# Loads of a batched residual matmul: two lines of a sample in one 8 KB piece, for four lines in one of 16 KB

## The chip, the cores and the metric

The kernel runs on one core of one Trainium2 chip. The metric is device time in microseconds of one execution of the whole program, the median of several; lower is better. The profile is of one such execution, recorded by the hardware profiler.

## The reference

There are 128 samples, each a matrix of 128 channels by 1024 points, and 8 weight matrices of 128 by 128, all in float32. Each sample has a subject number from 0 to 7. The sample is multiplied by its subject's weights, and the product is added to the sample.

```python
def reference(x, itok_B_0_7, L0_cond_weights):
    # x: (128, 128, 1024), itok_B_0_7: (128,) int32 in 0..7, L0_cond_weights: (8, 128, 128)
    w = L0_cond_weights[itok_B_0_7]
    return x + jnp.einsum('bct,bcd->bdt', x, w)
```

A sample is 512 KB, so the input and the output are 64 MiB each: every byte of them is read once and written once.

## The kernel before

**Tiles and slots.** The work is cut into 64 tiles of two samples (`G = 2`), 1 MB each. A tile lives in one of 23 slots of SBUF (`xs`, `SLOTS = 23`): the load fills the slot, the sum overwrites it in place, and the store reads it. A slot is therefore taken from the issue of its load to the landing of its store. Channels lie on the 128 partitions, so that a partition holds 4 KB of each sample.

**Loads.** SP issues them, two to a tile (L138, one for each sample), through the helper `transfer`, whose instruction carries the line L57. The sample in memory is 128 lines of 4 KB, one after the other. The load names them as 32 pieces of four lines (`ROWS = 4`, L142), so that one piece of 16 KB is contiguous in memory and is spread over four partitions. In the first 23 tiles the load of tile i waits until tile i-3 has landed (`LEAD = 3`, L136); later it waits until the store of the tile that had the slot before has landed (L134). A DMA that has landed adds 16 to its slot's semaphore, one from each of the 16 DMA engines.

**Arithmetic.** When both loads of a tile have landed, TensorE does eight matmuls of 128x128 by 128x512 into one of two PSUM buffers (L171). GpSimd copies each sample's weight matrix out of the eight on the chip ahead of time, by the subject number (L165). VectorE adds PSUM and the slot in one instruction for the tile (L181).

**Stores.** ACT waits for the sum and issues one store of 1 MB for the tile (L183, again with the line L57 of the helper). A store is 128 pieces of 8 KB on the side of SBUF: one partition's two samples lie side by side there. ACT does nothing else, so that a store waits only for its sum and for stores ahead of it on ACT's queue.

**Order.** There is no planner: each engine runs its own instructions in the order of the program, and semaphores tie them. Loads are on one hardware queue (SP's) and stores on another (ACT's); both feed the same 16 DMA engines. At the end SP waits for the last 23 stores (L192).

Of the kernel before, what the change touches and what calls it, by code (L numbers as in the profile page):

```python
# [1 line left out]

# [4 lines left out]

F32 = mybir.dt.float32
I32 = mybir.dt.int32
ALU = mybir.AluOpType


G = 2

N = 512  # L30

SLOTS = 23

W_SLOTS = 4
P_SLOTS = 2

R = 8
DMA = 16

TURN = DMA * (G + 1)  # L40

LEAD = 3

IDLE = 3

ROWS = 4
QUEUES = {mybir.EngineType.SP: "qSPDynamicHW", mybir.EngineType.Activation: "qActDynamicHW"}


def transfer(nc, engine, out, in_):  # L50

    later, nc._always_lower_symbolic_ap = nc._always_lower_symbolic_ap, False
    ins, outs = engine.lower_ap_dma(in_), engine.lower_ap_dma(out)
    nc._always_lower_symbolic_ap = later
    return engine.add_instruction(  # L57
        mybir.InstDMACopy(
            name=nc.get_next_instruction_name(),
            engine=engine.engine,  # L60
            ins=ins,
            outs=outs,
            mode="Copy",
            cce_op=ALU.bypass,
            queue=QUEUES[engine.engine],
        )
    )


@with_exitstack  # L70
def kernel(
    ctx: ExitStack,
    tc: tile.TileContext,
    x: bass.AP,
    subjects: bass.AP,
    weights: bass.AP,
    out: bass.AP,
):
    nc = tc.nc
    B, C, T = x.shape  # L80
    S, _, D = weights.shape
    NT = B // G

    def sbuf(name, *shape, dtype=F32):
        return ctx.enter_context(nc.sbuf_tensor(name, list(shape), dtype)).ap()

    given, near, wrap, index = (
        sbuf(name, 1, B, dtype=I32) for name in ("given", "near", "wrap", "index")
    )
    w_all = sbuf("w_all", C, S, D)  # L90
    ws = [sbuf(f"w{i}", C, 1, D) for i in range(W_SLOTS)]
    zeros = sbuf("zeros", C, N)
    xs = [sbuf(f"x{i}", C, G, T) for i in range(SLOTS)]
    ps = [
        ctx.enter_context(nc.psum_tensor(f"ps{i}", [D, G, T], F32)).ap() for i in range(P_SLOTS)
    ]

    s_given = tc.alloc_semaphore("s_given")
    s_wall = tc.alloc_semaphore("s_wall")
    s_index = tc.alloc_semaphore("s_index")  # L100
    s_zeros = tc.alloc_semaphore("s_zeros")
    s_copied = tc.alloc_semaphore("s_copied")
    s_product = tc.alloc_semaphore("s_product")
    s_added = tc.alloc_semaphore("s_added")
    s_slot = [tc.alloc_semaphore(f"s_slot{i}") for i in range(SLOTS)]

    with tc.tile_critical():  # L107

        nc.scalar.dma_start(given, subjects.rearrange("(o b) -> o b", o=1)).then_inc(s_given, DMA)

        nc.vector.memset(zeros, 0.0).then_inc(s_zeros, 1)  # L111
        nc.tensor.wait_ge(s_zeros, 1)
        for _ in range(IDLE):
            nc.tensor.matmul(  # L114
                ps[P_SLOTS - 1][:, G - 1, :N], zeros[:, :D], zeros, start=True, stop=True
            )

        nc.vector.wait_ge(s_given, DMA)  # L120
        nc.vector.tensor_scalar(near, given, -S, S - 1, ALU.max, ALU.min).then_inc(s_index, 1)  # L121
        nc.vector.wait_ge(s_index, 1)
        nc.vector.tensor_scalar(wrap, near, 0, S, ALU.is_lt, ALU.mult).then_inc(s_index, 1)  # L123
        nc.vector.wait_ge(s_index, 2)
        nc.vector.tensor_tensor(index, near, wrap, ALU.add).then_inc(s_index, 1)  # L125
        nc.gpsimd.wait_ge(s_index, 3)

        nc.sync.dma_start(w_all, weights.rearrange("s c d -> c s d")).then_inc(s_wall, DMA)  # L130
        for i in range(NT):
            k, turn = i % SLOTS, i // SLOTS
            if turn:
                nc.sync.wait_ge(s_slot[k], TURN * turn)  # L134
            elif i >= LEAD:
                nc.sync.wait_ge(s_slot[k - LEAD], DMA * G)  # L136
            for g in range(G):
                transfer(  # L138
                    nc,
                    nc.sync,  # L140
                    xs[k][:, g, :],
                    x[i * G + g].rearrange("(a r) t -> a (r t)", r=ROWS),  # L142
                ).then_inc(s_slot[k], DMA)

        nc.gpsimd.wait_ge(s_wall, DMA)
        for i in range(NT):
            k, turn = i % SLOTS, i // SLOTS
            p = ps[i % P_SLOTS]
            nc.tensor.wait_ge(s_slot[k], TURN * turn + DMA * G)
            if i >= P_SLOTS:  # L150
                nc.tensor.wait_ge(s_added, i - P_SLOTS + 1)
            for g in range(G):
                b = i * G + g
                if b % R == 0:
                    _, subject = nc.values_load_multi_w_load_instructions(
                        index[0:1, b : b + R],
                        engines=[mybir.EngineType.Pool],
                        min_val=0,
                        max_val=S - 1,
                        skip_runtime_bounds_check_because="the index is clamped on the chip above",  # L160
                    )
                w = ws[b % W_SLOTS]
                if b >= W_SLOTS:
                    nc.gpsimd.wait_ge(s_product, b - W_SLOTS + 1)
                nc.gpsimd.tensor_copy(w, w_all[:, bass.ds(subject[b % R], 1), :]).then_inc(  # L165
                    s_copied, 1
                )

                nc.tensor.wait_ge(s_copied, b + 1)
                for t in range(0, T, N):  # L170
                    mm = nc.tensor.matmul(  # L171
                        p[:, g, t : t + N],
                        w[:, 0, :],
                        xs[k][:, g, t : t + N],
                        start=True,
                        stop=True,
                    )
                mm.then_inc(s_product, 1)

            nc.vector.wait_ge(s_product, (i + 1) * G)  # L180
            nc.vector.tensor_tensor(xs[k], p, xs[k], ALU.add).then_inc(s_added, 1)  # L181
            nc.scalar.wait_ge(s_added, i + 1)
            transfer(  # L183
                nc,
                nc.scalar,
                out[i * G : (i + 1) * G].rearrange("g d t -> d g t"),
                xs[k].rearrange("d (o g) t -> d o (g t)", o=1),
            ).then_inc(s_slot[k], DMA)


        for i in range(NT - SLOTS, NT):
            nc.sync.wait_ge(s_slot[i % SLOTS], TURN * (i // SLOTS + 1))  # L192


# [1 line left out]
_INS = ["x", "itok_B_0_7", "L0_cond_weights"]  # L196
_OUTS = [((128, 128, 1024), "float32")]


# [20 lines left out]
```

## Time and profile before

| what | value |
|---|---|
| median of 3 runs | 327.43 us (327.18 to 327.75) |
| the profiled execution | 327.53 us |
| its span in the profile | 325.5 us |
| moved by DMA in the span | 134.85 MB, mean 414 GB/s |
| TensorE matmuls busy | 241.3 us, 74% of the span |
| VectorE busy | 147.9 us, 45% |
| GpSimd busy | 37.6 us, 12% |
| loads of x | 128 of 512 KB |
| stores | 64 of 1 MB |

The span reaches from the first instruction of the program to the last one in the profile; the execution's own time is 2.0 us longer, which lies outside. The page's slices cut the span into 40 equal parts of 8.1 us; a digit is the busy share of an engine in tenths. The trace also has a record for each DMA packet, with its queue, its size, its start and the time that it took: q1 is SP's queue and q10 ACT's. A packet of 4 bytes is the update of a semaphore. In the chain of waits, a line gives start, duration and what the time was spent on.

### The profile page before, as it was taken

How to read it: one execution, taken by the hardware profiler on the slowest of the kernel's cores; microseconds unless marked ns; L12 is line 12 of the kernel's file. 1: busy time of each engine (PE TensorE's matmuls, PEld its weight loads, DVE VectorE, ACT ScalarE, POOL GpSimd, SP SyncE). 2: the span in 40 equal slices, each digit the busy share in tenths (PEclk: the TensorE clock that was granted, in tenths of full speed). 3: DMA queues.
4: the chain of work that ended last, by engine and by line, in shares of the span. 5: the costliest groups of instructions: out<-in, count | busy, mean ns of one | idle time of the engine just before them, and what ended most of it. 6: DMA issues, size and time to landing. Idle time of an engine off the chain costs nothing.

```text
span 325.5 us, 1703 instructions
## 1 busy us (share of the span) xinstructions
PE 241.3 (74%) x518; PEld 95.2 (29%) x518; DVE 147.9 (45%) x68; POOL 37.6 (12%) x132
## 2 busy tenths in 40 slices
PE   6999998987989999989889889887777878000000
PEld 2444433332333333333333333332232332000000
DVE  1475765554555555555555555555354336100000
POOL 1111111111111111111111111111101110000000
PEclk9999999999999999999999999999999979755555
DMA  7999999999999999999999999999999999999994
GB/s 258 411 419 431 419 435 415 420 428 419 427 431 421 431 419 429 416 424 428 423 427 423 420 428 422 428 421 431 421 433 435 417 419 422 429 424 429 424 429 191
DMA packets 16410, 134.85 MB, mean 414 GB/s; under 512 B 3089, under 2 KB 4114, under 8 KB 4114
## 3 DMA queue, kind: packets, MB, share of 16 engines
q1 hardware_dynamic: 7184, 67.64, 49.6%
q10 hardware_dynamic: 9218, 67.11, 49.2%
q8 instruction: 4, 0.07, 0.1%
q14 instruction: 4, 0.03, 0.0%
HBM read 67.63 MB, written 67.11 MB: 414 GB/s over the span
## 4 chain that ended last, share of the span: by engine, by line
DMA 44%; SPq 23%; another core or an unknown queue 15%; PE 2%; issue 1%; DVE 1%
DMA x<-in_x_dram 29%; SPq L57 23%; DMA out_dram<-x 14%; PE ps L171 2%; DVE x L181 1%; SPq L130 0%; SPq L216 0%; SPq L107 0%
## 5 line engine op out<-in xcount | busy, mean ns | idle before, releaser
L171 PE MATMUL ps<-x,w 128*128 128x512 f32 x512 | 235.9, 607 | 32.5 <-DMA x<-in_x_dram 32.5
L181 DVE TENSOR_TENSOR x<-ps,x 128x2048 f32<-128x2048 f32 x64 | 146.7, 2292 | 128.0 <-PE ps L171 128.0
L171 PEld LDWEIGHTS ps<-x,w 128*128 128x128 f32 x512 | 93.4, 191 | 175.6 <-issue 97.3
L165 POOL COPY w<-w_all 128x128 f32 x128 | 37.4, 294 | 230.6 <-PE ps L171 224.6
L114 PE MATMUL ps<-zeros 128*128 128x512 f32 x6 | 5.4, 1076 | 1.7 <-DVE zeros L111 1.7
L114 PEld LDWEIGHTS ps<-zeros 128*128 128x128 f32 x6 | 1.8, 326 | 3.8 <-issue 2.1
L111 DVE MEMSET zeros<- 128x512 f32 x1 | 0.5, 485 | 1.1 <-SPq L107 1.1
L121 DVE TENSOR_SCALAR near<-given 1x128 int32<-1x128 int32 x1 | 0.2, 216 | 0.7 <-DMA given<-in_itok_B_dram 0.7
L125 DVE CUSTOM_DVE_ANT_0 index<-near,wrap 1x256 uint16<-1x256 uint16 x1 | 0.3, 280 | 0.0
L123 DVE TENSOR_SCALAR wrap<-near 1x128 int32<-1x128 int32 x1 | 0.2, 216 | 0.0
L207 POOL MEMSET const-float32-0.0<- 128x1 f32 x1 | 0.1, 98 | 0.2 <-issue 0.2
L207 POOL MEMSET const-bfloat16-1.0<- 128x1 bf16 x1 | 0.1, 101 | 0.0
L207 POOL MEMSET const-uint8-127<- 128x1 uint8 x1 | 0.1, 101 | 0.0
L207 POOL MEMSET const-float32-1.0<- 128x1 f32 x1 | 0.1, 98 | 0.0
## 6 DMA issues: line engine op xcount, KB each, us to landing
x<-in_x_dram SPq DMA_DIRECT2D x128, 512.0 KB, 11.8
out_dram<-x ACTq DMA_DIRECT2D x64, 1024.0 KB, 41.6
w_all<-in_L_cond_weights_dram SPq DMA_DIRECT2D x1, 512.0 KB, 4.4
given<-in_itok_B_dram ACTq DMA_DIRECT2D x1, 0.5 KB
```

The lines of the kernel that those rows point to most:

```text
L57: return engine.add_instruction(mybir.InstDMACopy(name=nc.get_next_instruction_name(), engine=engine.engine, ins=ins, outs=outs, mode="Cop ...
L111: nc.vector.memset(zeros, 0.0).then_inc(s_zeros, 1)
L114: nc.tensor.matmul(ps[P_SLOTS - 1][:, G - 1, :N], zeros[:, :D], zeros, start=True, stop=True)
L121: nc.vector.tensor_scalar(near, given, -S, S - 1, ALU.max, ALU.min).then_inc(s_index, 1)
L123: nc.vector.tensor_scalar(wrap, near, 0, S, ALU.is_lt, ALU.mult).then_inc(s_index, 1)
L125: nc.vector.tensor_tensor(index, near, wrap, ALU.add).then_inc(s_index, 1)
L165: nc.gpsimd.tensor_copy(w, w_all[:, bass.ds(subject[b % R], 1), :]).then_inc(s_copied, 1)
L171: mm = nc.tensor.matmul(p[:, g, t : t + N], w[:, 0, :], xs[k][:, g, t : t + N], start=True, stop=True,)
L181: nc.vector.tensor_tensor(xs[k], p, xs[k], ALU.add).then_inc(s_added, 1)
L207: nc = _bacc.Bacc("TRN2", target_bir_lowering=False, num_devices=1)
```

## The change

The constant `ROWS` goes from 4 to 2. A load then names a sample as 64 pieces of two lines, 8 KB each, and each piece is spread over two partitions. Issuing engine, queue, order, waits, slots and the number of loads stay as they are, and so do the stores and all arithmetic.

```diff
--- before
+++ after
@@ -43,7 +43,7 @@
 
 IDLE = 3
 
-ROWS = 4
+ROWS = 2
 QUEUES = {mybir.EngineType.SP: "qSPDynamicHW", mybir.EngineType.Activation: "qActDynamicHW"}
```

The only use of it is in the load's access pattern (L142), which is not edited:

```python
                    x[i * G + g].rearrange("(a r) t -> a (r t)", r=ROWS),
```

## The prediction

> **What bounds the kernel now.** I read the page's slices first, then the DMA queues over chosen stretches, then the end of the chain of waits. The slices:
>
> ```profile
> PE   6999998987989999989889889887777878000000
> DMA  7999999999999999999999999999999999999994
> GB/s 258 411 419 431 419 435 415 420 428 419 427 431 421 431 419 429 416 424 428 423 427 423 420 428 422 428 421 431 421 433 435 417 419 422 429 424 429 424 429 191
> ```
>
> DMA is full in every slice except the first and the last. TensorE's last six slices are empty: all multiplying is over at 275 us, and 50 us of stores follow. So no engine's arithmetic sets the end; it is set by how long 16 DMA engines take for 134.85 MB, and by whether they are ever left without work. The trace's packet records add up: the first data packet starts at 2.07 us, the packets of the two hardware queues took 321.6 us per DMA engine, the last one ends at 323.64, and the span closes at 325.5. 2.07 + 321.6 + 1.9 = 325.5: no idle time between.
>
> Next, who gets the DMA engines. q1 holds the loads (SP), q10 the stores (ACT). The queues over 30 to 210 us, and over 230 to 270 us:
>
> ```profile
> q1 hardware_dynamic: 4191, 45.82, 60.3%
> q10 hardware_dynamic: 4196, 30.48, 40.5%
> ...
> q10 hardware_dynamic: 1171, 8.54, 50.8%
> q1 hardware_dynamic: 771, 8.44, 50.0%
> ```
>
> The columns are packets, MB, share of the engines. In the first stretch the packets are equal (4191 and 4196) and the bytes are not (1.50 to 1). Per DMA engine a load of 512 KB is two packets of 16 KB and one of 4 bytes for the semaphore: 3 packets for 32 KB. A store of 1 MB is eight packets of 8 KB and one of 4 bytes: 9 packets for 64 KB. One packet each in turn gives 32/3 against 64/9, which is 1.50. So **turns go by packet, the semaphore's included**. In the second stretch the loads no longer have their turn every time: they have run 23 tiles ahead, SP waits for slots (L57 behind stores), and bytes are equal. That lead is the 50 us of stores at the end, and it hides the last tile's arithmetic, which the chain shows:
>
> ```profile
> 263.62 8.05 DMA x<-in_x_dram
> 271.67 0.04 issue
> 271.72 3.71 PE ps L171 x8
> ...
> 275.46 2.29 DVE x L181
> ```
>
> The last load lands at 271.67, its sum is done at 277.75, and its store waits in ACT's queue until 301.35.
>
> [...]
>
> **The change part by part.**
> (1) *Pieces.* Each load is 64 packets of 8 KB for 32 of 16 KB: 4096 more packets over the run, 256 per DMA engine. Bytes, partitions reached and semaphore packets stay. An 8 KB read isn't in the trace; the nearest row is the 8 KB store packet. Means over the run: 311.6 ns for it, 619.1 ns for a 16 KB load packet. 2 x 311.6 - 619.1 = 4 ns, times 256 = 1.0 us, all on the path, since DMA is full. Bounds: 0 if the cost goes by bytes (a 16 KB packet then stands for two of 309.5); 2 x 312.5 - 616.8 = 8.2 ns, 2.1 us, by the means of 30 to 210 us. [...] I take 1.0.
> (2) *Start.* Up to 18 us there are only loads, at 643 ns per 16 KB packet, 27 above that of 30 to 210 us. If that excess belongs to every packet, 22 more packets per engine cost 0.6 us; if to bytes, nothing; if it goes with shorter pieces, -0.6. I take 0 and keep both ends.
> (3) *Issue.* SP issues the same 128 loads (597 ns each, 77 of 325 us). The weight load of 1024 pieces took 0.44 us to issue, so more pieces cost SP nothing visible. ACT, VectorE, GpSimd and TensorE have the same instructions in the same order; no wait is added in the program.
> (4) *Turns.* This is the main term. A load becomes 5 packets for 32 KB per engine, 10 turns per tile, against 9 for the tile's store. With both queues full, stores now move 10/9 of the bytes of loads, not 2/3. Stores can't pass the loads that they depend on, so they catch up. At 18.3 us, when the first store packet runs, 5 tiles have landed; landing to store takes about 8 us (below), 1.6 tiles at 5 us a tile, so some 3.4 tiles of stores are behind. They gain one tile in nine: gone after about 31 of 64 tiles. From then on each store leaves as its tile is ready, loads have the rest, DMA stays full (two to three tiles of loads are always asked for by LEAD), and a tile takes each DMA engine 8 load and 8 store packets, 16 x 311.6 ns = 4.99 us. TensorE needs 3.43 us a tile and VectorE 2.29: neither binds.
> (5) *End.* The loads now finish late, and **the last tile's work is no longer covered**. From the last load packet to its store's first packet: 0.77 to land (270.90 to 271.67), 0.05 to start, 3.74 matmuls (271.72 to 275.46), 2.29 add, 0.03, and 1.1 from issue to first packet (weights: 0.97 to 2.07). Sum 7.98 us. Meanwhile DMA has the store before it, 2.49 us (8 x 311.6), and the rest of the one before that, which started two tiles (9.98 us) earlier, so 2.0 us before the loads ended, and had half the turns: 2.49 - 1.0 = 1.49. Idle: 7.98 - 2.49 - 1.49 = 4.0 us. Low end 3.2: if that store's first packet stood behind 1.5 us of load packets already taken up. High end 7.4: if TensorE's clock is at half for the last tile, as it was after a gap of 2.14 us at 262.56 (matmuls 0.85 us apart for 0.43: 8 x 0.42 = 3.4 more).
> Sum: 1.0 + 0 + 4.0 = +5.0 us: profiled span 330.5, profiled execution 327.53 + 5.0 = 332.5, and 0.1 less for a median of 327.43: **332.4 us**. Its own range is 330.0 (3.2 with pieces at no cost, 0.6 off at the start) to 335.
>
> **Rivals.**
> *Half clock at the end*, 0.13: as above, +3.4: 335.8. TensorE will pause about 1.5 us in every tile, as it did from 230 to 270, where the clock dipped once in eight tiles.
> *The backlog stays*, 0.11: the share is not by turns of single packets once pieces are equal (semaphore packets not counted gives 4 to 4 for equal bytes, no catching up), so stores stay 3 tiles behind and cover the last tile. Only (1) is left: 327.4 to 329.5, likeliest 328.4. Against it: 1.50 needs the semaphores to count; without them it would be 2.
> *Faster*, 0.06: [...] At 304 ns, 512 load pieces per engine save 512 x 5.5 = 2.8 us; it decides only with the backlog kept, since the 4.0 of the end outweighs it, and below some 308 ns (309.5 less 0.65 us over 512 packets): 324.6. For it: only the slower packets of the reads-only start. Against it: half-size store packets show no gain.
> *The piece stays whole or the queue cuts both alike* (no change): the page counts 4096 packets of 16 KB for the loads by difference, so the cut follows the access pattern; 0.02, in "same".
>
> **How the numbers follow.** Main case 0.68, half clock 0.13, backlog kept 0.11, faster 0.06, no change 0.02. Within 0.2% is 0.65 us, about what a measurement of this kernel can tell from no change. Slower: 0.68 + 0.13 + 0.08 of the backlog case = 0.89; same: 0.03 + 0.02 = 0.05; faster 0.06. The range for 8 in 10 goes from 329.3, below the main case and a little into the kept backlog, to 335.9, to the half clock.
>
> **What would show it.** Right: about 8190 load data packets of 8 KB at 310 to 316 ns; equal packets on q1 and q10 early with bytes near 0.9 to 1, then equal bytes; TensorE busy in slices nearly to the end at seven tenths; the last load landing near 319 us instead of 272; SP no longer waiting for stores; two gaps of DMA, about 1.5 and 2.5 us, in the last 12 us. Wrong: a last load before 300 us, or a last stretch of stores back to back; load packets off 308 to 316 ns would put (1) wrong; stores more than one tile behind in the second half would put (4) wrong.

## The result, and the profile after

The changed kernel takes 331.12 us (median of 4, 330.99 to 331.25) against 327.36 us for the kernel before: 3.76 us more, a ratio of 1.011 with a 95% interval of 1.0098 to 1.0122. The forecast was 332.4 us, slower. The profiled execution took 331.2 us with a span of 329.2, so 3.7 us more than the span before; what lies around the span is 2.0 us as before.

The slices of the page, after the change:

```profile
PE   6999667686776868777678677677677687686680
DMA  7999999999999999999999999999999999999964
GB/s 252 412 403 429 426 425 426 424 427 425 420 427 428 422 426 427 426 424 420 427 426 422 428 427 422 424 425 423 426 426 425 425 424 427 426 423 425 424 255 184
```

Up to the 38th slice DMA is as full as before and moves the same 425 GB/s. The loss is in the last two slices: 255 and 184 GB/s, where the kernel before had 429 and 191. TensorE has no empty slice until the last; it multiplies at six to eight tenths nearly to the end.

The queues of the changed kernel, as packets, MB and share of the engines, from 20 to 60 us and from 230 to 270 us:

```profile
q10 hardware_dynamic: 1223, 8.97, 53.2%
q1 hardware_dynamic: 1227, 8.07, 48.1%
...
q1 hardware_dynamic: 1303, 8.54, 51.0%
q10 hardware_dynamic: 1164, 8.49, 50.5%
```

At first the packets are equal again (1223 and 1227), and now the loads have fewer bytes: 8.07 to 8.97 MB, 0.90 to 1, the nine tenths that five packets for 32 KB against nine for 64 KB give. Later the bytes are equal and stores have fewer packets: they have caught up with the loads, and their queue is empty part of the time. A store now lands 9.6 us after its issue (median), where it was 41.6 before.

The end of the chain of waits (start, duration, what), and two short stretches from the table of windows (the stretch, its length, busy time of TensorE, weight loads, VectorE and GpSimd, clock, DMA share, GB/s):

```profile
277.56 39.79 DMA x<-in_x_dram
317.35 0.04 issue
317.39 3.71 PE ps L171 x8
321.11 0.02 issue
321.13 2.29 DVE x L181
```

```profile
317.00:319.60 2.60, 2.21 (x5) 1.06 (x6) 1.45 (x1) 0.00 (x0) 1.00 0.12 47
322.50:324.60 2.10, 0.00 (x0) 0.00 (x0) 0.92 (x1) 0.00 (x0) 1.00 0.00 0
```

The last load lands at 317.35 instead of 271.67. The durations of the matmuls and the sum behind it have not changed, but nothing covers them: while they run, DMA is nearly idle twice, at 47 GB/s and at 0. In the first of the two stretches data still move in one packet at a time from 317.46 on, until 319.32: a single engine is late, and the others have nothing to do. The store of the last tile is issued at 323.45 and its first packet starts at 324.66.

### The profile page after: what moved, and what is told of

It reads as the page before. It is cut to its first block, busy times and chain, and to the rows that moved or that the text cites. A ratio compares the mean times of both kernels' runs of the same rounds, so it can differ in the third digit from the quotient of the medians.

```text
span 329.2 us, 1703 instructions
## 1 busy us (share of the span) xinstructions
PE 240.7 (73%) x518; PEld 94.3 (29%) x518; DVE 147.9 (45%) x68; POOL 37.9 (12%) x132
## 4 chain that ended last, share of the span: by engine, by line
SPq 55%; DMA 39%; issue 1%; PE 1%; DVE 1%
SPq L57 55%; DMA x<-in_x_dram 39%; PE ps L171 1%; DVE x L181 1%; SPq L130 0%; SPq L216 0%; SPq L107 0%
## 6 DMA issues: line engine op xcount, KB each, us to landing
x<-in_x_dram SPq DMA_DIRECT2D x128, 512.0 KB, 35.1
```

## The experiments

Two theories stood against each other. **The lost lead**: with equal turns by packet, smaller load pieces let the stores catch up, so that no stores are left to cover the last tile's matmuls, sum and store. **The cost of pieces**: 4096 more packets make DMA itself slower, 3.7 us in all. Times are medians; ratios are against the kernel before, run on the same chip (327.47 to 327.64 us on the four chips of the experiments).

**1. Win the lead back without touching the loads.** Against the changed kernel, the store names SBUF without joining its two samples, so its pieces are 4 KB:

```diff
-                xs[k].rearrange("d (o g) t -> d o (g t)", o=1),
+                xs[k],
```

> Loads in 8 KB pieces as after the change, stores in 4 KB pieces. By turns of single packets, loads move 32 KB in 5 turns and stores 64 KB in 17, so bytes of loads to stores go 1.70 to 1 and loads run ahead again. Theory of the lost lead (the last tile's work is uncovered because stores catch up): a tail of stores comes back, the last load lands before 275 us, time 327.4 plus 0 to 2 us for the smaller store pieces. Rival, cost of pieces (each 4096 more packets cost 3.7 us of DMA time): at least 331.1, and up to 338 with 8192 more store packets.

Measured: 328.64 us, ratio 1.0029 (1.0019 to 1.0039), 2.5 us faster than the changed kernel although it has 8192 packets more. From 30 to 60 us the queues of this kernel were:

```profile
q1 hardware_dynamic: 1224, 8.04, 63.8%
q10 hardware_dynamic: 1219, 4.67, 37.9%
```

Equal packets, and bytes of 1.72 to 1 where turns give 1.70. The last load landed at 271.76 and a stretch of stores came back. That stretch ran at 421 GB/s from 280 to 320 us (426 in the kernel before), 1.2% less, so pieces of 4 KB have a small cost of their own. That fits the 1.1 us by which the run lies above the kernel before.

**2. Cover the end without touching any packet.** Against the changed kernel, stores are held back for a while near the end (`HOLD = 4`):

```diff
-            nc.scalar.wait_ge(s_added, i + 1)
+            held = max(i + 1, min(i + 1 + HOLD, 60)) if i >= 44 else i + 1
+            nc.scalar.wait_ge(s_added, held)
```

> Loads in 8 KB pieces; from tile 44 on a store is issued only when four more tiles are summed, and from the sum of tile 59 on all are released. This makes a backlog of stores just before the end and alters no packet. Lost lead: the backlog covers the last tile's work, 327.4 to 328.6 us (about 0.5 for a longer stretch of loads alone). Cost of pieces: 331 or more.

Measured: 328.18 us, ratio 1.0021 (1.0014 to 1.0028): 2.9 of the 3.8 us are back, with the same 8 KB packets. The last load landed at 303.07, and DMA worked through to its last packet at 324.13. What is left, 0.6 us, fits the stretch where loads run alone while the stores wait: 413 GB/s from 232 to 246 us, and 419 in the window of 230 to 270 us around it, where before it was 425:

```profile
232.00:246.00 14.00, 13.44 (x32) 6.03 (x33) 8.33 (x4) 2.06 (x7) 1.00 1.02 413
230.00:270.00 40.00, 38.57 (x91) 16.83 (x89) 25.20 (x11) 6.48 (x22) 1.00 1.01 419
```

Six parts in 425 of 40 us are 0.6 us.

**3 and 4. Lengthen the last tile's chain, with and without cover.** The last tile's eight matmuls (four in the program, each with two records in the trace) are done twice:

```diff
-                for t in range(0, T, N):
+                for t in [*range(0, T, N)] * (2 if i == NT - 1 else 1):
```

With 8 KB pieces: 

> Loads in 8 KB pieces, the last tile's eight matmuls are done twice (the same result is written again): 3.4 us more in the last tile's chain. Lost lead: that chain is on the path, 331.1 + 3.4 = 334.5 us, up to 338 if TensorE runs at half clock. Cost of pieces: DMA sets the end, 331.1.

With 16 KB pieces: 

> The kernel before (16 KB pieces) with the last tile's eight matmuls done twice. Both theories: 50 us of stores cover it, 327.4 us, within 0.2. A rise of 3.4 would put the reading of the tail wrong.

Measured: 334.48 us with 8 KB, ratio 1.0211 (1.0192 to 1.023), and 327.67 us with 16 KB, ratio 1.0004 (0.9995 to 1.0013). The chains show the same added work in both. First 8 KB, then 16 KB:

```profile
316.98 0.04 issue
317.03 7.15 PE ps L171 x16
324.18 0.02 issue
324.20 2.29 DVE x L181
```

```profile
271.77 0.04 issue
271.81 7.15 PE ps L171 x16
278.96 0.02 issue
278.99 2.29 DVE x L181
```

7.15 us instead of 3.71: 3.44 more. With 8 KB loads it lengthens the program by 3.4 us; with 16 KB loads more than 40 us of stores hide it. DMA sets the end in one kernel, the last tile's chain in the other.

**5. Shorten that chain.** Against the changed kernel, in the last tile alone each sample has its own wait, sum and store. This is the main part of the edit; the rest of it, left out here, gives the last tile's two loads semaphores of their own, on which TensorE waits sample by sample:

```diff
+            if i == NT - 1:
+                for g in range(G):
+                    b = i * G + g
+                    nc.vector.wait_ge(s_product, b + 1)
+                    nc.vector.tensor_tensor(
+                        xs[k][:, g, :], p[:, g, :], xs[k][:, g, :], ALU.add
+                    ).then_inc(s_added, 1)
+                    nc.scalar.wait_ge(s_added, i + 1 + g)
+                    transfer(nc, nc.scalar, out[b], xs[k][:, g, :]).then_inc(s_last[g], DMA)
+                break
```

> Loads in 8 KB pieces; in the last tile alone each sample has its own wait, sum and store. The chain behind the last load is shorter by four matmuls (1.7 us) and half an addition (1.15 us). Lost lead: 331.1 less 2.4 to 2.9, some 328.5 us. Cost of pieces: 331.1.

Measured: 328.59 us, ratio 1.0027 (1.0018 to 1.0036), as expected. The two sums of the last tile follow each other directly behind that of the tile before it, so that the gap of 2.3 us ahead of the last store is gone:

```profile
316.23 2.29 DVE x L195
318.52 1.13 DVE x L188
319.65 0.01 issue
319.66 1.23 DVE x L188
```

**6. Which half of the loads matters.** `r=2 if i < NT // 2 else 4` in the access pattern of the load: 8 KB pieces for the first 32 tiles, 16 KB for the others.

> The first 32 tiles are loaded in 8 KB pieces, the last 32 in 16 KB pieces. Lost lead: the second half wins it back (1.5 to 1 in bytes), the end is covered, 327.4 us plus up to 0.5. Cost of pieces as the cause: half of the change, 329.3.

Measured: 327.76 us, ratio 1.0004 (0.9994 to 1.0014). Half of the added pieces cost nothing that can be measured (the interval ends at 0.5 us); the second half of the run wins the lead back, and the last load lands at 291.23.

**7. Smaller still.** `ROWS = 1`.

> Loads in 4 KB pieces, one line each (ROWS = 1): 8192 more load packets than after the change. Turns: 9 for 32 KB against 9 for 64 KB, so stores are never behind for long. Lost lead: nothing more to lose, the same uncovered end as after the change, 331.1 us plus up to 1.3 for the pieces (8192 more store packets cost about 1 us in the run with 4 KB stores). Cost of pieces as the cause: 3.7 us per 4096 packets, 338.5.

Measured: 332.71 us, ratio 1.0147 (1.012 to 1.0174), 1.6 us above the changed kernel where up to 1.3 was expected and 7.4 by the cost of pieces. From 20 to 30 us:

```profile
q10 hardware_dynamic: 390, 2.82, 66.8%
q1 hardware_dynamic: 389, 1.43, 34.9%
```

Equal packets once more, bytes of 0.51 to 1 (turns give 0.50). From 30 to 300 us, the kernel before, the changed kernel and this one:

```profile
30.00:300.00 270.00, 213.83 (x462) 83.58 (x460) 134.08 (x59) 32.88 (x112) 0.96 1.01 425
30.00:300.00 270.00, 197.77 (x429) 76.94 (x428) 123.24 (x54) 31.70 (x107) 1.00 1.01 425
30.00:300.00 270.00, 205.18 (x427) 82.01 (x428) 123.13 (x54) 31.10 (x106) 0.96 1.02 422
```

422 GB/s for 425: 0.7% of 270 us is 1.9 us, about what this kernel lost. So a cost of pieces exists at 4 KB, and at 8 KB it is too small to be seen.

**8. Larger.** `ROWS = 8`: 32 KB pieces, tried twice, on two chips.

> Loads in 32 KB pieces (ROWS = 8), one packet and one semaphore packet per DMA engine and load. Turns: 32 KB in 2 against 64 KB in 9, bytes 2.25 to 1 until the slots are full. Lost lead: the end is covered as before the change, 327.4 us within 0.5. Cost of pieces as the cause: 2048 packets fewer than before, 325.6.

> The same kernel as in the run with 32 KB pieces, which came out at 400 us with packets of 1.7 us for 32 KB where two of 16 KB take 1.24. If that belongs to the piece: again 380 to 415 us and 32 KB packets well over 1.3 us, 2.2 us in the stretch with loads alone. If it was a disturbance of that run: 327 to 328 us and 1.24 us a packet, with the end covered as before the change.

Measured: 399.83 us, with executions from 385 to 412, and in the second run 392.86 us with a ratio of 1.199 (1.189 to 1.2087). Both theories missed this. It has to do with neither: the loads themselves are slow. The table of windows for the stretch with loads alone and for the next, second run, and then the same first stretch of the kernel before:

```profile
4.00:18.00 14.00, 11.01 (x19) 4.05 (x18) 2.29 (x1) 1.88 (x7) 0.88 1.11 264
20.00:60.00 40.00, 29.51 (x66) 11.41 (x65) 19.65 (x9) 4.70 (x16) 1.00 0.99 289
```

```profile
4.00:18.00 14.00, 13.14 (x28) 5.19 (x27) 4.58 (x2) 2.46 (x9) 1.00 1.04 418
```

DMA counts as full in both kernels, at 264 GB/s in one and 418 in the other. A packet of 32 KB took 2.2 us at first and 1.65 us over the run, where two of 16 KB take 1.24. Why is open.

**9. Drift between the DMA engines, and the issue of loads.** Each of the 16 DMA engines adds one to the slot's semaphore when its share of a load is done: the trace has 2064 updates of 4 bytes for the 129 loads of SP's queue, 16 each. In the changed kernel these updates for the last tile's two loads are spread over 10.1 us (307.26 to 317.35). I suspected the depth of the load queue, since the wait on the tile three before holds only for the first 23 tiles. Against the changed kernel:

```diff
-            elif i >= LEAD:
-                nc.sync.wait_ge(s_slot[k - LEAD], DMA * G)
+            if i >= LEAD:
+                j = i - LEAD
+                nc.sync.wait_ge(s_slot[j % SLOTS], TURN * (j // SLOTS) + DMA * G)
```

> Loads in 8 KB pieces; the wait for the landing of the tile three before (LEAD), which the kernel has for the first 23 tiles only, holds for all. No packet changes. After the change, the first DMA engine to finish a load and the last drift apart to 7 to 10 us in the second half, as loads lie 17 deep; with the wait, the spread should stay within some 2 us. If that drift costs time at the end, 0.5 to 1 us less than the changed kernel on the same chip; if only the uncovered chain of the last tile counts, the same within 0.2.

Beside it the changed kernel again: 

> The changed kernel itself, on the chip of the run beside it: 3.4 to 3.9 us above the kernel before.

Measured: 330.87 us, ratio 1.0102 (1.0086 to 1.0119), against 331.17 us, ratio 1.0107 (1.009 to 1.0124). The intervals overlap nearly whole, so no difference is shown. Nor did the spread close as expected: the updates for the last tile's loads came from 307.14 to 316.97, over 9.8 us. The depth of the queue is not what makes the engines drift, and what the drift costs was not tested.

The run settles another question. In the changed kernel SP is busier with issuing: 1514 ns for a load (median) where it was 597, and the page's chain of waits puts 55% of the span on it, for 23% before. With the added wait an issue takes 590 ns and a load lands 13.0 us after it, instead of 35.1, at the same time for the whole. So the issuing of loads is not what the change cost.

## Why the prediction was right, and where its sizes were off

The direction, the mechanism and the place were as forecast: turns by packet with the semaphore's packet counted, equal bytes later, a last load near 317 us (forecast 319), two idle stretches of DMA at the end. The sum came out at 5.0 for 3.7.

*Pieces, forecast +1.0.* This is the term that was mis-sized most. Up to 310 us the kernel before had moved 129.424 MB of samples and results, the changed one 129.375: 0.05 MB or 0.1 us. The packet records gave the wrong price. Their sum per DMA engine did rise, from 321.6 to 323.0 us, but the same bytes were moved in the same time: records of consecutive packets overlap by some nanoseconds, and with more packets there are more overlaps (3.1 us per engine before, 4.2 after). With overlaps counted once, the mean engine worked 318.5 us before and 318.8 after, from 2.07 us to the last packet. The prediction's opening sum, 2.07 + 321.6 + 1.9 with no idle time between, came out for the same reason: the overlaps hide idle time, 2.4 us per engine after 300 us, as the engines' last updates are 3.3 us apart (320.75 to 324.04). Experiment 7 shows a cost at 4 KB (422 GB/s for 425), and experiment 6 none above 0.5 us for half of the 8 KB pieces. The sign that the prediction gave for this term could not tell: load packets took 312.7 ns on average, inside its 310 to 316.

*Start, forecast 0.* The changed kernel had moved 5.48 MB at 18 us, the kernel before 5.51, 0.1 us; nothing of it was left at 180 us, when both had moved 74.18 MB.

*Issue, forecast 0.* Right for the time, by experiment 9. SP's median issue did go from 597 to 1514 ns, which was not forecast; it is 590 in experiment 9 with the same pieces and fewer loads in the queue, so it is not the pieces themselves.

*Turns.* Right: 0.90 measured for 0.90. Five such ratios agree with the rule or lie close: 1.50 before, 0.90 after, 1.72 for 1.70 with 4 KB stores, 0.51 for 0.50 with 4 KB loads, and 1.50 in the second half of experiment 6. The rival that left the semaphore's packet out needs 1.0 where 0.90 was found, and 2.0 where 1.72 was. Stores caught up earlier than after the 31 tiles forecast: loads and stores had 304 and 310 packets from 110 to 120 us, 333 and 287 from 120 to 130, when 23 stores had been issued.

*End, forecast +4.0 of idle DMA.* From the last load packet (316.54) to the last store's first (324.66) are 8.1 us, for 7.98 forecast. On the engine that finished last, 0.4 us of it were idle ahead of the last store but one and 2.3 ahead of the last, 2.7 together. The mis-sized step is the store two tiles back, which was taken to be 1.0 of 2.49 us done when the loads end: on that engine none of its eight packets had been moved by then, and it held DMA until 319.3, 2.8 us after the loads. Through the second half a store landed some 9 us after its issue, nearly two tiles. Over all 16 engines, idle time between 300 us and the last packet rose from 2.4 us to 5.8, by 3.4. Beside 2.3 and 2.4 us in the two gaps, 0.9 lies from 313 to 315 us (busy share 0.53), where engines that were ahead of the others had neither a load nor a store left to move; this third gap was not forecast. With 0.3 for the longer work of the mean engine, 0.1 of it for pieces by the bytes moved, the 3.4 make up the 3.7. The engine that finished last shows less idle time, 2.7, so it worked 1.0 us longer than the last one before the change. Experiment 9 did not find why engines fall behind, so this is open.

On the last engine, then, 4.0 of idle time and 1.0 of longer work were forecast, and 2.7 and 1.0 measured. That the second of these agrees is luck: it was put down to slower pieces, which the bytes moved do not show.

*The rivals.* Half clock: the granted clock stayed at 1.00 from 300 to 325 us, through the last matmul; not seen. The kept backlog and the faster pieces: refuted by the queues, which show stores catching up, and by 425 GB/s in both kernels; the faster case took an estimate of mine, 304 ns for a load packet, where 312.7 were measured. That the cut would not happen: the page counts 4096 load packets more. Experiments 1 to 5 settle the cause: each change that gave cover back or shortened the chain took 2.5 to 2.9 us off with the 8 KB load pieces kept, and the 3.4 us put into the chain came out whole.

No version beat the kernel before: it keeps DMA full until its engines finish, one after the other, in the last 3.3 us, and what was tried at best reaches that again.

## What to carry to other kernels

In these runs, when two queues shared full DMA engines, the size of the packets on each decided who got the bandwidth (1.50 to 1 in bytes with loads in 16 KB, 0.90 to 1 in 8 KB, at equal packets): work out bytes per turn, with one packet for the semaphore, before changing a piece's size. Where loads led, the surplus of stores at the end covered the last tile's latency (3.44 us more of matmuls left the time at 327.67 us, ratio 1.0004); where stores kept up, that latency was added to the program (the same 3.44 us cost 3.4), and a shorter last tile or a few stores held back won back 2.5 to 2.9 us of the 3.8 that the change cost. Read a cost of packets from bytes moved by a given time (0.05 MB less by 310 us here), not from the packets' own durations (1.4 us more per engine).

## What the runs showed that was not expected

- Pieces of 32 KB: 1.65 us on average against 1.24 for two of 16 KB, and 393 us for the whole kernel. Pieces of 16 and 8 KB move the same 425 GB/s in the body, 4 KB loads 422.
- DMA's busy share says nothing of this: it was over 0.98 at 264, 289 and 425 GB/s.
- Loads alone were slower than loads and stores together: 413 GB/s from 232 to 246 us in experiment 2, and 418 from 4 to 18 us in the kernel before, against 425 from 30 to 300 us.
- The 16 DMA engines drifted apart: the updates for the last tile's two loads lie within 2.8 us in the kernel before (268.89 to 271.67), within 10.1 us after the change (307.26 to 317.35). The last store of the changed kernel, which had the engines to itself, has its 16 updates within 0.2 us (327.51 to 327.70).
